# Layer 3's windowed-attention block: order of the weights' scaling, the norm's root and its product, the last steps and the leaving sequences

## The chip, the cores and the metric

The kernel runs on one core of one Trainium2 chip. The metric is the device time of the whole program in microseconds, as the median of several runs. Five engines run side by side, each through its own list of instructions in a fixed order: TensorE (PE: matrix products and transposes, with weight loads shown as PEld), VectorE (DVE), ScalarE (ACT), GpSimd (POOL) and SyncE (SP, which issues transfers). An instruction starts when the one ahead of it on its engine and the results that it needs are done.

## The reference

Four layers, each a half-step of a feed-forward block, an attention, and the feed-forward block again. The change lies in the feed-forward block of layer 3, called twice (ahead of that layer's attention and behind it). It works on 2 x 1024 tokens of 128 features, in two passes (DEPTH = 2):

```
h = shift_token(x)                              # features 64.. come from the token before
q, k, v = split(h @ wqkv)                       # 8 heads of 64
q, k = rotary_xpos(l2norm(q) * qs, l2norm(k) * ksc)
o = local_attention(q, k, v)                    # windows of 64 tokens, each sees the one before
x = x + o @ wo
h = shift_token(x)
h = (h - mean(h)) / sqrt(var(h) + 1e-05) * lg + lb
a, g = split(h @ w1 + b1)
x = x + (a * gelu(g)) @ w2 + b2
```

After it, the outer program adds half of the block's result to its own x.

## The kernel before

`l3_ffn(w3, tag, first, rb)` (line 1900) is one call of the block; `first` is true for the call ahead of the attention. A **unit** is one pass over one of four sequences of 512 tokens, so there are 8 units, and a unit has four **steps** of 128 tokens: 32 steps (`n_steps`). The loop at line 2231 runs `n` from -2 to 37. In each round it goes through six **places**, and at each place it runs one part for an earlier step, its lag:

| place | part (lag) | engines |
|---|---|---|
| 0 | `project` (0): products `p_qk`, `pv`; square `sq`, the rotary products `t`, the roots of the norms (10 small instructions on POOL), the scaled keys | PE, ACT, DVE, POOL |
| 1 | `to_features` (2): transposes `pt_qk`, copies `qT` (ACT) and `kT` (DVE) | PE, ACT, DVE |
| 2 | `exponentials` (4): eight exponentials with sums `sm` | ACT, DVE |
| 3 | `weights` (3): scores `ps3`, mask `s`, row maximum `nm` | PE, DVE |
| 4 | `with_values` (6): product `po3`, copy `oT` | PE, DVE |
| 5 | `turn_weights` (5): transposes `pt3`, copy `PT` | PE, ACT |

`shares(n - 5)` (line 2049) scales the exponentials by the reciprocal of their sum on POOL (L2051); `turn_weights` needs its result. It stands at place 0, behind what `later` holds for that place.

`later` is a table written by hand: what a unit still has to do after its four steps, as (round counted from the unit's first step, place). The list `parts` (line 2213) fills it: `summed` (10, 2), `shifted` (10, 3), `centred` (11, 1), `squared` (11, in the middle of the exponentials), `variance` (12, 0), `spread_by_act` (12, in the middle of the exponentials), `normed` (13, 0), three `hidden` (13, 2), `close_unit` (14, 0) and `leave` (14, 1). `MIDST` is the key of what `exponentials` runs behind its third exponential.

The norm of a unit goes so. `variance` brings the sums of squares to `rs` (a copy on DVE) and takes the root in two POOL instructions (L230 and L233). `spread_by_act` multiplies the identity by `rs` in four ACT instructions, tile `dg`. `normed` multiplies `dg` by a matrix of equal numbers on PE (`pb`), which spreads the factors over the partitions, and one DVE instruction scales `h` by it. `hidden` multiplies `h` by `w1`, in three pairs of products (`pag`), each followed by a Gelu (`ge`, ACT) and a product (`hh`, DVE). `close_unit` multiplies `hh` by `w2` (`pz`).

PSUM is held in three pairs of banks (tag "d": `p_qk`, `pt_qk`, `ps3`, `pt3` and each `pag`) and two single banks (tag "m": `pv`, `pb`, `pm`, `pvar`, `po3`, `pz`, `pt_y`, `pt_z`), each tag in turn. PE's, ACT's and the named POOL instructions are kept in the order of the program; DVE's order inside these calls is chosen by the scheduler when the kernel is built.

Rounds 32 to 37 hold no `project`: they drain the lags. The last unit's own steps (`rest`, line 2243) follow the loop, in the first call spread between those of the attention.

A sequence leaves with `leave(b)` (line 2181): transposed back, added to x, and in the first call normalized for the attention by `leave_normed` (line 349). That puts three tasks on a chain: statistics, scaling to `y`, and after a gap counted in places (`gap`, here 3) the transposes `pt_y` (`turn`, line 319). `tick()` at the end of each place runs what is due.

Of the kernel before, what the change touches and what calls it, by code (L numbers as in the profile page):

```python
# [115 lines left out]
def tile_macaron(ctx, tc, x_in, const_in, vec_in, w0_in, ws_in, ws3_in, w2f_in, w3_in, out):  # L116
# [82 lines left out]
    def mm_in_order(dst, lhsT, rhs, start=True, stop=True):  # L199
        tc.keep_in_program_order(nc.tensor.matmul(dst, lhsT=lhsT, rhs=rhs, start=start, stop=stop))  # L200
# [130 lines left out]
    def chain(b):  # L331
        parts = deque()
        chains.append([b, clock[0], parts])
        return lambda gap, f, products=True: parts.append((gap, f, products))
# [7 lines left out]
    def tick(busy=False):  # L342
        clock[0] += 1
        for c in list(chains):
            while c[2] and clock[0] >= c[1] + c[2][0][0] and not (busy and c[2][0][2]):
                busy |= c[2][0][2]
                run(c)

    def leave_normed(b, spare, gap, pinned=False, start=1, to_route=True):

        st = []

        def scale():
            scaled(y, x, b, st[-1] if pinned != "parts" else st[0][1:], pinned is True)
            ready.add(b)

        if pinned == "parts":
            got, halves = statistics_in_parts(x, b)
            st.append(got)
            spare(start, halves[0], False)  # L360
            spare(1, halves[1], False)
            spare(2, scale, False)
        else:
            spare(start, lambda: st.append(statistics(x, b)), False)
            spare(1, scale, False)
        spare(gap, lambda: turn(b))
        if routed and to_route:
            spare(1, lambda: logits(b))
            if b % 2:
                first, second, third = route(b // 2)  # L370
                spare(1, first, False)
                spare(routed["gaps"][0], second)
                spare(routed["gaps"][1], third)
# [1521 lines left out]

    MIDST = 2.5

    def l3_ffn(w3, tag, first, rb):  # L1900
        with pool(tag) as sb, banks(tag + "ps", d=3, m=2):
            units = [(l, b) for l in range(2) for b in range(B)]
            n_steps = TB * len(units)
# [12 lines left out]
            def W(l, name):  # L1916
                return W3(w3, f"{name}{l}")
# [39 lines left out]
            def project(step):  # L1957
                u, t = step // TB, step % TB
                l, b = units[u]
                h = u_state[u]["hT"][:, ts(t, P)]  # L1960
                p = pair("p_qk")
                mm_in_order(p[:, 0:512], h, W(l, "wq"))
                mm_in_order(p[:, 512:1024], h, W(l, "wk"))
                pv = bank("m", "pv3")
                mm_in_order(pv, h, W(l, "wv"))

                sq = sb.tile([P, 16, 64], F32, tag="sq", name="sq")
                act(sq.rearrange("p h d -> p (h d)"), p, AF.Square)
                tab = W(l, "tab").rearrange("p (t f i d) -> p t f i d", t=TB, f=2, i=2)[:, t]
                t1 = sb.tile([P, 16, 64], F32, tag="t1", name="t1", bufs=3)  # L1970
                t2 = sb.tile([P, 16, 64], F32, tag="t2", name="t2")
                by_head = lambda v: v.rearrange("p (i h) d -> p i h d", i=2)
                over = lambda v: v[:, :, None, :].to_broadcast([P, 2, 8, v.shape[2]])
                p3 = p.rearrange("p (h d) -> p h d", d=64)
                vector.tensor_mul(by_head(t1), by_head(p3), over(tab[:, 0]))
                for half in range(2):
                    a, z = ts(half, 32), ts(1 - half, 32)
                    vector.tensor_mul(by_head(t2[:, :, a]), by_head(p3[:, :, z]), over(tab[:, 1, :, a]))
                rn = sb.tile([P, 16], F32, tag="rn", name="rn", bufs=6)
                vector.tensor_reduce(rn, sq, AX.X, ALU.add)  # L1980
                pool_in_order(nc.gpsimd.tensor_add(t1, t1, t2))  # L1981
                inverse_root(sb, rn, rn, "ir16", ALU.max, 1e-24, nc.gpsimd, pin=pool_in_order)
                pool_in_order(nc.gpsimd.tensor_mul(t1[:, 8:16, :], t1[:, 8:16, :], bcast(rn[:, 8:16], 64)))
                v = sb.tile([P, S], F32, tag="v", name="v", bufs=7)
                act_copy(v, pv)

                vb = sb.tile([P, S], F32, tag="vb", name="vb", bufs=6) if t else vbs[u % 2]
                nc.sync.dma_start(vb[64:128], v[0:64])
                if t:
                    nc.sync.dma_start(vb[0:64], s_state[step - 1]["v"][64:128])  # L1990
                s_state[step] = {"qk": t1, "rn": rn, "v": v, "vb": vb}
# [42 lines left out]
            def exponentials(step):  # L2034

                midst = later.pop((step + 4, MIDST), ())
                s, nm, rn = (s_state[step][v] for v in ("s", "nm", "rn"))
                sm = sb.tile([P, 8], F32, tag="sm", name="sm", bufs=2)
                for i in range(8):
                    si = s[:, i, :]  # L2040
                    h = 2 * (i % 4) + i // 4
                    act(si, si, AF.Exp, bias=nm[:, i : i + 1], scale=rn[:, h : h + 1], accum_out=sm[:, i : i + 1])
                    if i == 2:
                        for f, u in midst:
                            f(u)
                vector.reciprocal(sm, sm)
                s_state[step]["sm"] = sm

            def shares(step):
                s = s_state[step]["s"]  # L2050
                pool_in_order(nc.gpsimd.tensor_mul(s, s, bcast(s_state[step].pop("sm"), P)))  # L2051
# [102 lines left out]
            def hidden(u, c, at=whole):  # L2154
                l, b = units[u]
                a, n = HCH[c]
                h2, w1, m = u_state[u]["h2"][:, at], W(l, "w1"), at.stop - at.start
                if c == 0 and at.start == 0:
                    u_state[u]["hh"] = rb.tile([P, 3, S], F32, tag="hh", name="hh")
                pg, pa = two_banks("pag")  # L2160
                mm_in_order(pg[:n, :m], w1[:, HID + a : HID + a + n], h2)
                mm_in_order(pa[:n, :m], w1[:, a : a + n], h2)
                ge = tmp("ge")
                act(ge[:n, :m], pg[:n, :m], AF.Gelu, bias=W(l, "b1g")[:n, c : c + 1])
                vector.scalar_tensor_tensor(
                    u_state[u]["hh"][:n, c, at], pa[:n, :m], W(l, "b1a")[:n, c : c + 1], ge[:n, :m], ALU.add, ALU.mult
                )
# [13 lines left out]
            def leave(b, at=whole):  # L2181
                pt = bank("m", "pt_z")
                t0, n = at.start // P, (at.stop - at.start) // P
                for t in range(n):
                    transpose_in_order(pt[:, ts(t, P)], yT[:, b, ts(t0 + t, P)])
                tiles = slice(b * TB + t0, b * TB + t0 + n)
                xb = x[:, tiles, :].rearrange("p t d -> p (t d)")
                vector.scalar_tensor_tensor(xb, pt[:, : n * P], 0.5, xb, ALU.mult, ALU.add)
                if first:
                    leave_normed(b, chain(b), 3)  # L2190
                else:
                    nc.sync.dma_start(out[:, tiles, :], x[:, tiles, :])

# [16 lines left out]
            if first:  # L2210
# [2 lines left out]
            parts = [  # L2213
                (summed, 10, 2), (shifted, 10, 3), (centred, 11, 1), (squared, 11, MIDST), (variance, 12, 0),
                (spread_by_act, 12, MIDST),
                (normed, 13, 0), *((lambda u, c=c: hidden(u, c), 13, 2) for c in range(3)), (close_unit, 14, 0),
                (lambda u: leave(units[u][1]) if units[u][0] else None, 14, 1),
            ]
            later, last = {}, len(units) - 1
            for u in range(len(units)):  # L2220
                for f, after, place in parts[: -1 if u == last - 1 else None] if u < last else ():
                    if u == last - 1 and f is close_unit:
                        after, place = 13, 5
                    if u == last - 1 and f is spread_by_act:
                        f, place = spread, 2
# [3 lines left out]
            if first:  # L2229
                later.setdefault((8, 1), []).append((scale_layer, 1))  # L2230
            for n in range(-2, n_steps + 6):
                for place, (part, lag) in enumerate((
                    (project, 0), (to_features, 2), (exponentials, 4), (weights, 3), (with_values, 6), (turn_weights, 5)
                )):
                    for f, u in later.pop((n, place), ()):
                        f(u)
                    if place == 0 and 0 <= n - 5 < n_steps:
                        shares(n - 5)
                    if 0 <= n - lag < n_steps:
                        part(n - lag)  # L2240
                    tick()
            assert not later, later
            rest = [attended, mean, variance, spread, normed]
# [15 lines left out]
    with pool("ws") as wp:  # L2259
# [9 lines left out]
        with pool("l2x") as l2x:  # L2269
# [20 lines left out]
            with ExitStack() as first_layer:  # L2290
# [3 lines left out]
                with pool("l1v", side="right") as vb:  # L2294
# [4 lines left out]
                    project, roots, unit_norm = projection(xb, seqs)  # L2299
# [206 lines left out]
```

## Time and profile before

| | us |
|---|---|
| median of 3 runs (2608.64 to 2609.08) | 2608.88 |
| the profiled run's own time | 2606.24 |
| its span, first to last instruction | 2604.3 |
| PE busy in the span | 2236.7 (86%) |
| DVE busy | 1771.5 (68%) |
| ACT busy | 1334.8 (51%) |
| POOL busy | 945.4 (36%) |

The mean granted TensorE clock is 0.909. Times of instructions are read from the span's start. The first call's first projection of a full pipeline is at about 1555 us, its last `pag` of the loop at 1883 us; the second call's loop has its last `pag` at 2570 us. PE's busy time comes from matmuls whose ends are modelled, since they are pipelined; so one may seem to start a little before the one ahead of it ends. "Idle before" is the time for which an engine stood ahead of an instruction, and the name behind the arrow is what released it.

### The profile page before, as it was taken

The page shows a single profiled execution, that of the slowest core. Times are in us where ns is not written, and L with a number is a line of the kernel's source. Part 1 is how long each engine was busy: PE and PEld are TensorE (multiplying, and loading weights), DVE is VectorE, ACT ScalarE, POOL GpSimd, SP SyncE. Part 2 cuts the span into 40 slices and gives each one's busy share as a digit, 9 for nine tenths or more (in the row PEclk, how much of TensorE's full clock was granted, in tenths as well). Part 3 has the DMA queues.
Part 4 walks back from the last instruction along what each step waited for, and adds up shares of the span by engine and source line. Part 5 has one row for each costly group of instructions (what it writes and reads, how often), then busy time and mean ns, then how long its engine had stood idle before and what let it go on. Part 6 is the DMA issues. An engine that isn't in the chain of part 4 may idle for free.

```text
span 2604.3 us, 50971 instructions
## 1 busy us (share of the span) xinstructions
PE 2236.7 (86%) x19070; PEld 1276.6 (49%) x19070; DVE 1771.5 (68%) x4755; ACT 1334.8 (51%) x3271; POOL 945.4 (36%) x1519
## 2 busy tenths in 40 slices
PE   5578679988778998988768868999889999799997
PEld 2246334443344444458647845555533333456555
DVE  3755667777466777755655579888557775788874
ACT  4056205444443544434425338887615555588884
POOL 2023113233233222333422368777310000787761
PEclk9789789899689999889978879999889999899999
DMA  3052000000000000037325721110000000110100
GB/s 150 0 170 92 1 0 2 2 1 2 1 1 1 2 2 5 17 128 238 106 83 159 252 84 28 24 24 21 3 1 1 1 1 1 29 28 22 24 22 13
DMA packets 40142, 113.21 MB, mean 43 GB/s; under 512 B 7064, under 2 KB 16536, under 8 KB 39384
## 3 DMA queue, kind: packets, MB, share of 16 engines
q1 hardware_dynamic: 36520, 100.94, 12.2%
q0 software_dynamic: 2944, 6.04, 1.1%
q8 instruction: 151, 2.47, 0.4%
q10 hardware_dynamic: 432, 2.98, 0.3%
q14 instruction: 95, 0.78, 0.1%
HBM read 79.78 MB, written 15.47 MB: 37 GB/s over the span
## 4 chain that ended last, share of the span: by engine, by line
PE 59%; DVE 18%; POOL 11%; ACT 6%; issue 4%; DMA 2%; SPq 0%; POOLq 0%; DVEq 0%; ACTq 0%
PE pk_at L200 11%; PE po_at L200 6%; PE pa L200 4%; PE pq_at L200 4%; DVE t L184 3%; PE pz L200 3%; PE pag L200 3%; PE pe L200 3%; PE po L200 2%; PE idle L200 2%; PE pt L197 2%; DVE y L184 2%; POOL t L1981 2%; PE pg L200 2%; PE p_qk L200 2%
## 5 line engine op out<-in xcount | busy, mean ns | idle before, releaser
L940 ACT ACTIVATE PT<-pk_at 128x512 f32<-128x512 f32 (+3 forms) x768 | 335.3, 488 | 377.6 <-PE pq_at L200 240.3
L200 PE MATMUL pk_at<-qx,km 32*128 32x512 f32 (+3 forms) x1536 | 400.6, 559 | 5.9 <-ACT PT L940 3.0
L184 DVE CUSTOM_DVE_ANT_0 s<-pq_at,cst 128x384 f32<-128x384 f32 (+3 forms) x512 | 249.3, 487 | 98.9 <-PE pq_at L200 46.2
L200 PE MATMUL pq_at<-km,qT 32*128 32x128 f32 (+3 forms) x1024 | 274.6, 504 | 15.6 <-DVE nm L184 12.5
L1923 ACT ACTIVATE s<-s,nm,rn 128x128 f32<-128x128 f32 x512 | 245.7, 483 | 4.4 <-DVE nm L184 4.2
L943 POOL TENSOR_SCALAR_AFFINE_SELECT PT<-PT 128x256 f32<-128x256 f32 x256 | 104.7, 411 | 383.5 <-ACT PT L940 382.3
L200 PEld LDWEIGHTS pk_at<-qx,km 32*128 32x128 f32 x1536 | 146.9, 191 | 155.0 <-issue 90.8
L200 PE MATMUL po_at<-PT,vh 128*32 128x128 f32 (+3 forms) x2432 | 203.3, 393 | 3.8 <-POOL PT L943 3.7
L184 DVE TENSOR_REDUCE nm<-pq_at 128x1 f32<-128x512 f32 x256 | 164.7, 684 | 52.5 <-PE pq_at L200 51.1
L184 DVE TENSOR_TENSOR t<-p_qk,w 128x512 f32<-128x512 f32 (+1 forms) x192 | 155.1, 861 | 53.5 <-ACT sq L1923 51.1
L1981 POOL TENSOR_TENSOR t<-t,t 128x1024 f32<-128x1024 f32 x64 | 151.2, 2362 | 55.9 <-DVE t L184 45.1
L200 PE MATMUL pq_at<-km,t 32*128 32x512 f32 x512 | 163.7, 657 | 0.1
L200 PE MATMUL p_qk<-w,hT 128*128 128x512 f32 x256 | 135.2, 654 | 18.1 <-DVE hT L184 9.2
L2051 POOL TENSOR_TENSOR s<-s,sm 128x1024 f32<-128x1024 f32 x64 | 121.5, 1899 | 63.1 <-DVE sm L184 62.1
L200 PEld LDWEIGHTS po_at<-PT,vh 128*32 128x32 f32 x2432 | 54.1, 110 | 169.9 <-issue 121.8
L233 POOL TENSOR_TENSOR ln_r<-ir,minus_half 128x4 f32<-128x4 f32 x60 | 62.0, 1034 | 202.4 <-DVE ir L184 200.5
L200 PEld LDWEIGHTS pq_at<-km,qT 32*128 32x128 f32 x1024 | 110.4, 190 | 43.6 <-DVE nm L184 23.1
L324 ACT COPY yT<-pt_y 128x512 f32<-128x512 f32 x56 | 32.7, 585 | 181.5 <-PE pt_y L197 181.2
L197 PE MATMUL pt<-ident,s 128*128 128x128 f32 x640 | 94.0, 294 | 31.1 <-POOL s L2051 28.5
L1585 POOL DMA_INDIRECT xg<-yd,come x60 | 57.4, 957 | 174.3 <-PE pt_x L197 74.3
L184 DVE SCALAR_TENSOR_TENSOR y<-pe,g,y 128x128 f32<-128x128 f32 x240 | 80.8, 348 | 30.7 <-PE pe L200 24.5
L197 PE MATMUL pt_y<-ident,y 128*128 128x128 f32 x224 | 48.6, 344 | 60.6 <-DVE y L184 47.2
(444 smaller groups left out, 5301.8 us busy)
## 6 DMA issues: line engine op xcount, KB each, us to landing
wf<-in_w2f_dram SPq DMA_DIRECT2D x45, 836.0 KB, 4.7
vb<-v SPq DMA_DIRECT2D x112, 128.0 KB, 2.3
w<-in_w2f_dram SPq DMA_DIRECT2D x15, 836.0 KB, 8.7
skew<-qe SPq DMA_DIRECT2D x16, 512.0 KB, 4.9
rel<-skew SPq DMA_DIRECT2D x64, 128.0 KB, 3.4
od<-o SPq DMA_DIRECT2D x60, 64.0 KB, 5.3
w<-in_w_dram SPq DMA_DIRECT2D x1, 3200.0 KB
w<-in_w_dram SPq DMA_DIRECT2D x12, 173.0 KB, 9.0
```

Source lines behind the costliest of these rows:

```text
L184: i = op(*args, **kw)
L197: return nc.tensor.transpose(dst, src, ident[: src.shape[0], : src.shape[0]])
L200: tc.keep_in_program_order(nc.tensor.matmul(dst, lhsT=lhsT, rhs=rhs, start=start, stop=stop))
L233: pin(nc.gpsimd.tensor_tensor(dst, v, minus_half[:, :n], ALU.pow))
L324: by_order(nc.scalar.copy(yT[:, b, :], pt))
L940: by_order(nc.scalar.activation(PT[:, i, q0:], pk[:, q0:], AF.Exp, scale=SC8))
L943: nc.gpsimd.affine_select(d, d, pattern=[[0, 2], [1, P]], base=0, channel_multiplier=-1, compare_op=ALU.is_ge, fill=0.0)
L1585: nc.gpsimd.indirect_dma_start(xT[s], None, yds[k][:, :], bass.IndirectOffsetOnAxis(ap=come[:, i : i + 1], axis=0))
L1923: tc.keep_in_program_order(nc.scalar.activation(*args, **kw))
L1981: pool_in_order(nc.gpsimd.tensor_add(t1, t1, t2))
L2051: pool_in_order(nc.gpsimd.tensor_mul(s, s, bcast(s_state[step].pop("sm"), P)))
```

## The change

There are six edits, all in or for `l3_ffn`.

1. `shares(n - 5)` is run ahead of what `later` holds for place 0, so ahead of `variance` and its root.
2. `normed` gets a key of its own, `BEHIND`: it runs inside `project`, behind its three products; in a round without `project`, at the end of place 0.
3. `exponentials` runs `squared` behind the third exponential as before, and `spread_by_act` behind the fourth.
4. In the rounds from 32 on, `turn_weights` is run at place 4 and `with_values` at place 5.
5. `leave_normed` is called with a gap of 9 places, not 3.
6. `BEHIND = 0.5` is defined.

```diff
-    MIDST = 2.5
+    MIDST, BEHIND = 2.5, 0.5
...
                 pv = bank("m", "pv3")
                 mm_in_order(pv, h, W(l, "wv"))
+                for f, v in later.pop((step, BEHIND), ()):
+                    f(v)
...
-                    if i == 2:
+                    if i == (2 if midst and midst[0][0] is squared else 3):
                         for f, u in midst:
                             f(u)
...
                 if first:
-                    leave_normed(b, chain(b), 3)
+                    leave_normed(b, chain(b), 9)
...
-                (normed, 13, 0), *((lambda u, c=c: hidden(u, c), 13, 2) for c in range(3)), (close_unit, 14, 0),
+                (normed, 13, BEHIND), *((lambda u, c=c: hidden(u, c), 13, 2) for c in range(3)), (close_unit, 14, 0),
...
             for n in range(-2, n_steps + 6):
+                ends = [(with_values, 6), (turn_weights, 5)]
                 for place, (part, lag) in enumerate((
-                    (project, 0), (to_features, 2), (exponentials, 4), (weights, 3), (with_values, 6), (turn_weights, 5)
+                    (project, 0), (to_features, 2), (exponentials, 4), (weights, 3), *ends[:: 1 if n < n_steps else -1]
                 )):
+                    if place == 0 and 0 <= n - 5 < n_steps:
+                        shares(n - 5)
                     for f, u in later.pop((n, place), ()):
                         f(u)
-                    if place == 0 and 0 <= n - 5 < n_steps:
-                        shares(n - 5)
                     if 0 <= n - lag < n_steps:
                         part(n - lag)
+                    elif part is project:
+                        for f, u in later.pop((n, BEHIND), ()):
+                            f(u)
                     tick()
```

## The prediction

> **What bounds the kernel now.** I read the busy time by stretch first. The change touches only the two calls of `l3_ffn` (about 1512 to 1900 us and 2217 us to the end), and in both a unit of four steps takes 42.05 us.
>
> ```profile
> core 0: us, PE busy (x) PEld busy (x) DVE busy (x) ACT busy (x) POOL busy (x), PEclk, DMA share, GB/s
> 1656.00:1698.00 42.00, 40.68 (x390) 24.91 (x384) 36.45 (x51) 34.73 (x93) 31.20 (x56) 1.00 0.10 23
> ```
>
> TensorE is busy for 40.68 of 42.00 us at full clock. So a unit ends when PE has done its list, and only what opens or closes a gap on PE counts: 1.32 us per unit can be won at most. The chain that ended last, in order of time, shows what releases PE there:
>
> ```profile
> 1664.66 1.88 POOL s L2051
> ...
> 1666.59 1.09 PE pt L197 x8
> ...
> 1671.42 2.41 DVE t L184 x3
> ...
> 1673.97 3.67 PE pag L200 x8
> ```
>
> PE waits for the scaled weights (`s`, L2051), then for the projections' readers (`t`) before `pag`. The timeline of that stretch (start, duration, idle before) gives the rows for the sum:
>
> ```profile
> 1663.62 1.04 POOL L233 TENSOR_TENSOR rs<-ir,minus_half 128x4 f32<-128x4 f32 x1
> ...
> 1664.63 1.90 POOL L2051 TENSOR_TENSOR s<-s,sm 128x1024 f32<-128x1024 f32 x1
> ...
> 1665.71 1.27 ACT L1923 ACTIVATE dg<-ident,rs 128x128 f32<-128x128 f32 x4
> ...
> 1666.59 1.09 PE L197 MATMUL pt<-ident,s 128*128 128x128 f32 x8 [0.72 <-POOL s L2051]
> ...
> 1666.78 0.68 DVE L184 COPY kT<-pt_qk 128x512 f32<-128x512 f32 x1
> ...
> 1667.51 1.02 PE L200 MATMUL pb<-dg,onesm 128*128 128x512 f32 x2
> ...
> 1668.37 1.88 PE L200 MATMUL p_qk<-w,hT 128*128 128x512 f32 x4
> ...
> 1669.27 0.99 ACT L1926 COPY PT<-pt 128x1024 f32<-128x1024 f32 x1
> ...
> 1670.34 1.02 ACT L1923 ACTIVATE sq<-p_qk 128x1024 f32<-128x1024 f32 x1
> ...
> 1670.61 0.74 DVE L184 SCALAR_TENSOR_TENSOR h<-h,w,pb 128x512 f32<-128x512 f32 x1
> ...
> 1671.40 2.42 DVE L184 TENSOR_TENSOR t<-p_qk,w 128x1024 f32<-128x1024 f32 x3
> ...
> 1671.83 1.88 PE L200 MATMUL pag<-h,w 128*128 128x512 f32 x4
> ...
> 1673.97 3.67 PE L200 MATMUL pag<-h,w 128*128 128x512 f32 x8 [0.26 <-DVE t L184]
> ```
>
> The 1.32 us are 0.72 (weights), 0.26 (`pag`) and 0.34 (`pvar`). Note that `h` ends at 1671.35, in the shadow of `sq`, and that ACT has no pause from 1664.27 to 1670.26.
>
> **Part 1: weights ahead of the root (POOL).** POOL is free at 1663.26 (end of L1983's product), and `sm` is there since 1661.92. Now the weights run 1663.35 to 1665.25, 1.28 us earlier, and the root's two instructions 1665.34 to 1666.65, 1.99 later. PE can turn the weights as soon as `po` ends, 1665.87: the 0.72 us go. What is late next is `p_qk`. There are three pairs of banks, and a step takes four, so `p_qk` gets the pair of the `pt_qk` before it, which `kT`'s copy releases at 1667.46. `p_qk` starts at about 1667.55 instead of 1668.37.
>
> **Part 2: the root's product behind the projections (PE, DVE).** `pb` takes 0.87 us of PE from ahead of `p_qk` to behind `pv`. Together: 1667.55 + 1.72 + 0.87 + 0.87 = 1671.0 for `pt_qk`, which began at 1670.96 before. The gain of part 1 is already spent there, on the wait for `kT`.
>
> **Part 3: the spread after four exponentials (ACT).** `dg` waits for the root. The fourth exponential leaves ACT free at 1666.20; the root is there at 1666.65, so `dg` starts at about 1666.70: ACT stands for 0.5 us. Queued behind that wait are four exponentials, the copy `PT`, the square `sq`, the copies `v` and `qT`, the table load and the Gelu. `PT` moves from 1669.27 to 1669.78. `sq` follows 0.91 behind it (0.89 in the step before, 1661.38 to 1662.27), at 1670.69, and ends at 1671.71.
>
> **What it does to `h`.** In the changed program as built, VectorE holds, in this order: `nm`, the first product of `t`, then `h`, then the other two of `t`. Before, `h` stood ahead of all three. `t` never starts before `sq` has ended (1671.36 to 1671.40 here). So: `t`'s first product 1671.75 to 1672.95 (1.22 us by the groups by form), `h` until 1673.6, and `pag`, which reads `h`, at about 1673.72 instead of 1671.83. PE stands from 1672.0 to 1673.72. `pag`'s twelve matmuls take 5.42 us unbroken (row at 2535.93 in the last unit), end 1679.14 against 1677.64: **+1.5 us per unit**. Behind `pag` PE has no wait before 1701.19, so nothing takes this back; the Gelu and `hh` keep ahead of `pz` (before by 1.4 us). Cheaper bound: if `dg` never waits, `sq` ends at 1671.18, and the same steps give +1.0. Dearer bound: +2.0, if the root is 0.5 us later still. I take 1.5, since every term has a row. Steps with both projections and `pb` occur for units 0 to 4, in two calls: 10 x 1.5 = **+15 us** (10 to 20).
>
> The weights pass only the root's two instructions on POOL, and the moved steps issue no DMA, so SP's queue stays as it is. The two transfers of `v` follow its copy, and are read six steps later.
>
> **Part 4: drain of the first call, and the leaving sequences.** The dear place is the step before the drain:
>
> ```profile
> 1823.61 1.04 POOL L233 TENSOR_TENSOR ln_r<-ir,minus_half 128x4 f32<-128x4 f32 x1
> ...
> 1824.69 1.12 DVE L184 TENSOR_SCALAR y<-x,ln_mv,ln_r 128x128 f32<-128x128 f32 x4 [3.99 <-POOL ln_r L233]
> ...
> 1825.09 1.24 PE L197 MATMUL pt_y<-ident,y 128*128 128x128 f32 x4 [5.09 <-DVE y L184]
> ...
> 1826.85 0.68 DVE L184 COPY oT<-po 128x512 f32<-128x512 f32 x1
> ```
>
> With the gap 9 instead of 3 `pt_y` goes one step later, and `p_qk` no longer stands behind it: it runs at 1819.85. But the wait moves. `pm` takes the bank of the `po` before it, free only after `oT` (1827.53), which stands behind `y` on DVE. So PE waits 5.1 us before `pm`, and queued behind it are `pt_qk`, `ps` and `po`. What is won is on DVE: `t` starts at 1827.6 instead of 1830.19, and POOL's chain with it (2.6 us). Next, the weights in front of the root: `pm` and `pt_qk` run slow until 1831.0 (1.72 each), then `qT`'s copy, three exponentials, the square (1833.0 to 1833.6) and five exponentials until 1836.0, so `sm` is there at 1836.5; the weights run 1836.7 to 1838.6 (before 1840.61 to 1842.51); `pt` 1838.65, `po` until 1840.7, the root 1838.7 to 1840.0, `dg` until 1841.3, `pb` 1841.4, `h` until 1843.1, `pag` 1843.25 to 1848.65. Before it ended at 1853.45: -4.8. In the last steps `po` goes behind `pt`; `pvar` still starts at the same distance, `pag` gains 0.1, and `pz` ahead of the last `po` 0.4. **-5.3 us** in all. Bounds: -8 (the whole 5.09 wait, and the slow clock behind it), 0 (each wait turns up again). The leavings inside the attention that follows show no wait of PE before `pt_y` (1935.45): 0, within 1 either way.
>
> **Part 5: drain of the second call.** There is no `pt_y`. Weights end 1.28 earlier, at 2530.3, but `po` now stands between `pt` and `pb`, and `dg` ends 2.0 later, at 2533.0: `pb` at 2533.6 (2533.38 before), `pag` 0.5 earlier thanks to the clock, then 0.15 and 0.4 as above: **-1.1 us** (-3 to +1).
>
> **The clock.** PE stands for 1.75 us before `pag`. Does it come back slow?
>
> ```profile
> 1563.85 1.09 PE L197 MATMUL pt<-ident,s 128*128 128x128 f32 x8 [1.70 <-POOL s L2051]
> ...
> 1842.57 1.97 PE L197 MATMUL pt<-ident,s 128*128 128x128 f32 x8 [3.02 <-POOL s L2051]
> ```
>
> After 1.70 us eight transposes take 1.09, after 3.02 us 1.97, and the next product 1.71 (2533.38) instead of 1.02. After a wait of 2.23 us (1876.30) the `po` rows are slow too. So the step lies between 1.7 and 2.23, and I take 0, with +1.6 per unit as the other end. [...]
>
> **Sum.** 15 - 5.3 - 1.1 = +8.6 us. The profiled run took 2606.24 us (span 2604.3 and 1.94 around it), 2.6 under the median 2608.88; taken from the median: **2617.5 us**.
>
> **Rivals.**
> - *The wait is only taken away (faster).* `pag` starts when PE is ready for it, 1672.0, and not when `h` is. Then a unit wins 0.2 (twelve at 5.42 end 1677.4); with no wait for `kT` either, up to 1.0. -10 x 0.2 - 6.4 = -8.4: 2600.5. It decides if `t`'s first product starts before 1670.0. For it: `p_qk` ends 0.8 us earlier. Against: `sq` stands behind ACT's unbroken row. 0.11.
> - *The drain gives nothing.* The stall goes from `pt_y` to `pm` in full: +15, 2624. For it: `oT` is the same row. Against: `t` and POOL's chain don't wait for `pm`. 0.15.
> - *PE comes back slow ten times:* 1.6 x 10 more, 2633. The gap is near 1.73 us (2560.58), where `pvar` kept its 1.05. 0.07.
> - *The unit's loss is half* (root early, `h` sooner): 0.7 a unit, 2609.5. 0.12.
>
> **How the numbers follow.** The forecast has 0.55, and its own range is 2612 to 2623. No change means within 0.2%, 5.2 us, about what a measurement here can tell: 2603.7 to 2614.1. The half loss and a little of the forecast fall in it, 0.16; faster 0.11, the first rival; slower 0.73. Range 2607 to 2627: it takes in the drain's rival and the half loss, and leaves out the first rival and the slow clock, 0.18.
>
> **What would show it.** Right: in a unit, the wait of `pt` for `s` gone, a wait of about 0.6 before `p_qk`, about 1.75 before `pag` with `h` as releaser, `dg` idle 0.5 for `rs`, units of 43.5 us, and `pm` at about 1827 (shifted by five units' loss, some 7.5 us) waiting for `oT`. Wrong: `pag` without wait for `h`, or units under 42.

## The result, and the profile after

| | before | after |
|---|---|---|
| median of 7 runs each, side by side, us | 2608.88 (2603.35 to 2611.57) | 2618.92 (2615.58 to 2624.02) |
| ratio, 95% interval | | 1.0042, 1.0032 to 1.0053 |
| the profiled run, us | 2606.24 | 2619.29 |
| PE, DVE, ACT, POOL busy, us | 2236.7, 1771.5, 1334.8, 945.4 | 2237.6, 1777.1, 1333.7, 945.3 |

The changed kernel is slower by 0.42%, 10 us; the forecast was 8.6. PE's work is the same and no engine's grew by more than 0.4%. So what is lost is waiting, and the page's list of costliest groups names the place. Its last two columns are busy time and mean of one, then the idle time of the engine just ahead of the group and what ended it:

```profile
L200 PE MATMUL pag<-h,w 128*128 128x512 f32 (+3 forms) x204 | 94.2, 615 | 17.7 <-DVE h L184 17.7
```

TensorE stands 17.7 us ahead of `pag`, and all of it is ended by `h` on VectorE; before it was 4.2 us in all, 1.7 of it ended by `h`. A steady unit in the busy time by stretch, 43.4 us instead of 42.05 and at full clock:

```profile
core 0: us, PE busy (x) PEld busy (x) DVE busy (x) ACT busy (x) POOL busy (x), PEclk, DMA share, GB/s
1655.00:1698.40 43.40, 40.97 (x384) 25.10 (x383) 36.66 (x51) 34.78 (x92) 31.21 (x57) 1.00 0.10 22
```

The chain of waits in that unit, in order of time (start, us, what). It no longer runs over POOL's `s` and `pt`, but over ACT's row and two VectorE instructions:

```profile
1664.65 1.82 ACT s L1923 x8
1666.47 0.98 ACT PT L1926
1667.45 0.93 ACT sq L1923
...
1668.40 1.22 DVE t L184
1669.63 0.67 DVE h L184
```

The timeline of the same step (start, duration, work, idle before):

```profile
1662.70 1.06 PE L197 MATMUL pt<-ident,s 128*128 128x128 f32 x8
...
1663.37 1.28 ACT L1923 ACTIVATE dg<-ident,rs 128x128 f32<-128x128 f32 x4 [0.26 <-POOL rs L233]
...
1664.33 1.99 PE L200 MATMUL p_qk<-w,hT 128*128 128x512 f32 x4 [0.57 <-DVE kT L184]
...
1667.02 1.02 PE L200 MATMUL pb<-dg,onesm 128*128 128x512 f32 x2
...
1668.40 1.22 DVE L184 TENSOR_TENSOR t<-p_qk,w 128x1024 f32<-128x1024 f32 x1 [0.31 <-ACT sq L1923]
...
1669.55 0.73 DVE L184 SCALAR_TENSOR_TENSOR h<-h,w,pb 128x512 f32<-128x512 f32 x1
...
1670.43 5.39 PE L200 MATMUL pag<-h,w 128*128 128x512 f32 x12 [1.51 <-DVE h L184]
```

`pt` no longer waits for `s`; `p_qk` waits 0.57 for `kT`, `dg` 0.26 for the root, and `pag` 1.51 for `h`. `pb` was done by 1668.04, yet `h` started at 1669.55: it stood behind `t`'s first product.

To compare kernels stage by stage I take the time from the start of one `pag` to the start of the next; the opening runs from a call's first `p_qk` to its first `pag`. "After, again" is a second profile of the changed kernel, from a later run, and "gap alone" an experiment told below.

| stage, us | before | after | after, again | gap alone |
|---|---|---|---|---|
| first call: opening | 115.72 | 117.49 | 118.98 | 115.70 |
| four units | 168.21 | 173.65 | 173.71 | 168.22 |
| last unit to the drain's first `pag` | 49.75 | 45.05 | 44.95 | 44.90 |
| to the drain's second `pag` | 35.43 | 36.59 | 37.58 | 35.28 |
| attention, to the next `p_qk` | 334.28 | 336.78 | 333.54 | 336.18 |
| second call: opening | 108.70 | 111.89 | 110.61 | 109.35 |
| four units | 168.22 | 175.26 | 173.74 | 168.22 |
| drain's first `pag` | 41.56 | 41.01 | 41.07 | 41.55 |
| drain's second `pag` | 34.36 | 34.71 | 34.83 | 34.36 |
| to the end | 33.99 | 35.47 | 35.56 | 33.98 |

The openings, the attention and the first drain's second `pag` differ by 1 to 3 us between two profiles of one kernel; units and the drains' first `pag` repeat to 0.1 us, apart from the second call's first unit in "after", which is 1.6 us longer (below). I rest on these, and on the ratios.

### The profile page after: what moved, and what is told of

It is laid out like the page before. It is cut to its first block, busy times and chain, and to the rows that moved or that the text cites. A ratio compares the mean times of both kernels' runs of the same rounds, so it can differ in the third digit from the quotient of the medians.

```text
span 2617.4 us, 50964 instructions
## 1 busy us (share of the span) xinstructions
PE 2237.6 (85%) x19070; PEld 1276.9 (49%) x19070; DVE 1777.1 (68%) x4755; ACT 1333.7 (51%) x3271; POOL 945.3 (36%) x1519
## 4 chain that ended last, share of the span: by engine, by line
PE 56%; DVE 20%; ACT 9%; POOL 7%; issue 4%; DMA 3%; SPq 0%; POOLq 0%; ACTq 0%; DVEq 0%
PE pk_at L200 11%; PE po_at L200 6%; PE pq_at L200 4%; PE pag L200 4%; DVE t L184 3%; PE pa L200 3%; PE pz L200 3%; ACT s L1923 3%; PE po L200 3%; PE pe L200 2%; DVE y L184 2%; PE p_qk L200 2%; DVE s L184 2%; ACT sq L1923 2%; PE pg L200 2%
## 5 line engine op out<-in xcount | busy, mean ns | idle before, releaser
L200 PE MATMUL pag<-h,w 128*128 128x512 f32 (+3 forms) x204 | 94.2, 615 | 17.7 <-DVE h L184 17.7
```

## The experiments

The kernels ran on several chips, on which the kernel before took 2609 to 2622 us; in the profiles the first call began between 1509 and 1530 us. So totals are given as ratios to runs of the kernel before on the same chip; the unit is the length that most units of the profile have. Names beginning with a are the changed kernel with one thing put back or moved, and with b the kernel before with one thing added.

| kernel | unit, us | ratio to before, 95% interval |
|---|---|---|
| before | 42.05 | |
| edit 1 alone (b_shares) | 43.55 | 1.0053, 1.0039 to 1.0067 |
| all but edit 2 (a_product_first) | 42.53 | 1.0000, 0.9988 to 1.0012 |
| all but edit 1 (a_root_first) | 43.04 | 1.0049, 1.0036 to 1.0061 |
| all (after, again) | 43.43 | 1.0036, 1.0020 to 1.0052 |
| all, `h` ahead of `t` (pin_h) | 42.56 | 1.0011, 1.0002 to 1.0020 |
| all, product ahead of `pv` (a_between) | 42.36 | 1.0006, 0.9994 to 1.0019 |
| all but edit 4 (a_order_back) | 43.43 | 1.0040, 1.0027 to 1.0053 |
| edit 5 alone (b_gap) | 42.05 | 0.9973, 0.9963 to 0.9984 |
| edit 4 alone (b_drain) | 42.06 | 1.0018, 1.0009 to 1.0028 |
| edits 4 and 5 (b_gap_drain) | 42.05 | 1.0009, 0.9997 to 1.0021 |
| edit 5, and 1 in the drains (b_gap_sh32) | 42.05 | 0.9982, 0.9971 to 0.9993 |
| edit 5, and 1 in the second drain (b_gap_sh2) | 42.07 | 0.9976, 0.9964 to 0.9989 |

### What the unit loses

**pin_h**: `h` and the instructions of `t` pinned in the order of the program, in the steps that hold both. The excerpt shows the first of `t`'s instructions; the others, the sums `rn` and `h` are held in the same way.

```diff
+                behind = later.pop((step, BEHIND), ())
+                hold = tc.keep_in_program_order if behind else lambda i: i
...
-                vector.tensor_mul(by_head(t1), by_head(p3), over(tab[:, 0]))
+                hold(vector.tensor_mul(by_head(t1), by_head(p3), over(tab[:, 0])))
```

> The changed kernel, with one thing put back: on VectorE the scaling of h stands ahead of t's three products again, in the five units of each call where both meet; no other engine's list changes. Theory (h stands behind t's first product, and the square comes late; both count): pb ends at 1667.9, so h runs 1668.05 to 1668.8 and t from 1668.85 instead of 1668.40; pag no longer waits for h, but its second pair waits for t until about 1671.4, where it now starts at 1672.2. A unit takes 42.6 us instead of 43.41, and the time is about 2611 (10 x 0.8 less than 2618.9). Rival 1 (h's place is no matter, the late root sets pag): units stay at 43.4, 2619. Rival 2 (h's place is all of the loss): units at 42.05 or less, 2605 or less.

Measured: 42.56, and 1.0011. That is the theory's 42.6, and neither rival's. The place of one 0.73 us instruction in VectorE's list is worth 0.85 us a unit. The rest is that `t` now waits for `h`, and that the second pair of `pag` then waits for `t`:

```profile
1681.09 0.75 DVE L184 SCALAR_TENSOR_TENSOR h<-h,w,pb 128x512 f32<-128x512 f32 x1
1681.75 2.41 DVE L184 TENSOR_TENSOR t<-p_qk,w 128x1024 f32<-128x1024 f32 x3
...
1684.31 1.95 PE L200 MATMUL pag<-h,w 128*128 128x512 f32 x4 [0.37 <-DVE t L184]
```

**a_between**: the product runs behind `p_qk` and ahead of `pv`. The scheduler puts `h` ahead of `t` by itself.

```diff
+                for f, v in later.pop((step, BEHIND), ()):
+                    f(v)
                 pv = bank("m", "pv3")
                 mm_in_order(pv, h, W(l, "wv"))
-                for f, v in later.pop((step, BEHIND), ()):
-                    f(v)
```

> The changed kernel with the root's product one place further ahead: behind p_qk, but ahead of pv. Theory: nothing of PE's is later than now, but pb is done 0.9 us earlier, VectorE holds h ahead of t's three products again and runs it in the shadow of the square; t starts when the square is done, as it does now. pag's first pair starts behind pt_qk, its second when t has ended: units of 42.2 us, about 2 us under the changed kernel in the first call per two units, 11 to 12 us under it in all (10 units x 1.2). Rival 1 (t, not h, sets pag): 43.4. Rival 2 (as with h pinned): 42.56.

Measured: 42.36, between the 42.2 expected and pin_h; 9.7 us under the changed kernel on the same chip. In one step of its timeline the square runs from 1669.66 to 1670.67, `h` from 1670.10 to 1670.84 and `t` from 1670.83; `pag` starts at 1671.04 without a wait, and only its later products wait for `t`, 0.45 us. So the place of `h` costs no more, and what is left over the kernel before (0.31) fits the later square; no run takes that away alone.

**a_product_first**: edit 2 undone.

```diff
-                (normed, 13, BEHIND), *((lambda u, c=c: hidden(u, c), 13, 2) for c in range(3)), (close_unit, 14, 0),
+                (normed, 13, 0), *((lambda u, c=c: hidden(u, c), 13, 2) for c in range(3)), (close_unit, 14, 0),
```

> The changed kernel with edit 2 undone: the root's product stands ahead of the projections again, the rest stays (weights ahead of the root, dg behind the fourth exponential). Theory: h goes back ahead of t on VectorE without a pin; pb waits about 0.3 us for dg, p_qk starts 1.2 us later, but the square stands behind ACT's own list until 1667.45 anyway, so t is not later; pag's second pair starts at about 1671.0 instead of 1672.2. A unit takes 42.2 us, the time is about 2607. Rival (the product behind the projections saves PE time, so that undoing it costs): units over 43.4, above 2619.

Measured: 42.53, and no difference from before. The unit is shorter than the changed kernel's, as expected, but by 0.9 and not 1.2 us, since `pb` waited 0.94 us for `dg` and not 0.3, and the square came behind `p_qk`.

**a_root_first**: edit 1 undone.

```diff
-                    if place == 0 and 0 <= n - 5 < n_steps:
-                        shares(n - 5)
                     for f, u in later.pop((n, place), ()):
                         f(u)
+                    if place == 0 and 0 <= n - 5 < n_steps:
+                        shares(n - 5)
```

> The changed kernel with edit 1 undone: the root ahead of the weights again, the product still behind the projections, dg behind the fourth exponential. Theory: pt waits some 0.7 us for s again, hidden for the most part in p_qk's wait for kT; dg finds its root ready and the square comes 0.3 us earlier; h still stands behind t's first product. A unit takes 43.1 us; the time is about 2616 to 2618, as the first call's drain loses some 1 us of its gain. Rival (the weights in front are the whole loss, since the root is late): units at 42.1, about 2606.

Measured: 43.04 (43.1 expected). The total was worse than expected, no better than the changed kernel's: its second drain took 43.17 us to the first `pag` instead of 41.01. So the late root is not the whole loss in the unit, and the rival falls.

**b_shares**: the reverse of that edit, in the kernel before.

> The kernel before with edit 1 alone, in all rounds: the weights ahead of the root; the root's product still ahead of the projections, dg behind the third exponential. Theory: pt's wait of 0.72 us goes, but dg waits about 1 us for the root, pb waits for dg ahead of p_qk, and the square and t come 0.5 to 1 us later: units of 42.6 to 42.9 instead of 42.05; both drains gain 1.0 (weights 1.28 earlier). 4 to 7 us over before. Rival (the wait is only taken away): units of 41.4, 7 us under before.

Measured: 43.55, worse than the theory's 42.6 to 42.9, and 1.0053. The timeline says where the estimate was short:

```profile
1665.15 1.28 ACT L1923 ACTIVATE dg<-ident,rs 128x128 f32<-128x128 f32 x4 [0.73 <-POOL rs L233]
...
1666.49 1.13 PE L200 MATMUL pb<-dg,onesm 128*128 128x512 f32 x2 [0.94 <-ACT dg L1923]
...
1674.08 1.10 PE L200 MATMUL pag<-h,w 128*128 128x512 f32 x2 [1.19 <-DVE t L184]
```

The wait of 0.72 for `s` turned into 0.73 on ACT, 0.94 on PE ahead of `pb`, and 1.19 ahead of the second pair of `pag`. So putting the weights in front costs the unit 1.50 by itself. With the weights in front, edit 3 (`dg` behind the fourth exponential) takes 1.02 of that away (43.55 to 42.53; the drains' edits leave the unit as it is), and edit 2 adds 0.88 again (42.53 to 43.41), by `h`'s place on VectorE. But these prices don't add up one by one: edits 2 and 3 without edit 1 cost 0.99 (a_root_first), and all three together 1.37. Neither edit 2 nor edit 3 was run alone.

### What the drains win and lose

**b_gap**: one number.

```diff
-                    leave_normed(b, chain(b), 3)
+                    leave_normed(b, chain(b), 9)
```

> The kernel before with edit 5 alone: the gap of 9 places. Theory: it is the whole of the first drain's gain and costs nothing elsewhere. Units 42.05; from the last full unit's pag to the one in the drain (steps 28 to 33 of the first call) 46.4 us, where before took 49.74; from there to the next pag 35.4 as before (b_gap_drain: 35.98); second call as before (41.55 and 34.36). 3.4 us under before. Rival (the stall only moves to pm): 49.7, no difference.

Measured: 44.90 where 46.4 was expected (before 49.75), then 35.28; 6.9 us under before. The rival (the stall only moves) falls, though the wait itself is there as predicted, at `pm`, and as long as it was at `pt_y`:

```profile
1828.10 2.05 PE L200 MATMUL pm<-h,onesm 128*128 128x512 f32 x2 [5.10 <-DVE nm L184]
...
1840.48 1.09 PE L197 MATMUL pt<-ident,s 128*128 128x128 f32 x8 [0.66 <-POOL s L2051]
```

The last row tells where the gain comes from. In the kernel before, this `pt` came 44.57 us behind the last unit's `pag`, after a wait of 3.02 us (the prediction's row at 1842.57); now it comes at 42.07, since `t` and POOL's chain are earlier. That is 2.50 us. And behind the wait of 0.66 `pt`, `pb` and `pt_qk` take 1.09, 1.06 and 1.04 us, where they took 1.97, 1.92 and 1.91 behind the 3.02, at a granted clock of 0.50 (1842.57 to 1847.00). That is the other 2.35.

No kernel of the study is faster than this one edit; the two below that add to it can't be told from it.

**b_drain**: edit 4 alone.

```diff
-                    (project, 0), (to_features, 2), (exponentials, 4), (weights, 3), (with_values, 6), (turn_weights, 5)
+                    (project, 0), (to_features, 2), (exponentials, 4), (weights, 3), *ends[:: 1 if n < n_steps else -1]
```

> The kernel before with edit 4 alone: from round 32 on pt ahead of po. Theory: po (1.8 us of PE) no longer fills the wait for the scaled weights, PE stands 4.4 instead of 3.0 us ahead of pt and po follows at slow clock. First call 49.7 and then 36.0 to 36.6 (before 35.43), second call 44.1 (before 41.55) and 35.5 (before 34.36): 4 to 5 us over before. Rival (as predicted: pvar at the same distance, pz earlier): 0.5 us per call under before.

Measured: 50.28 and 36.68 in the first call, 44.01 and 35.52 in the second; 1.0018, 5.6 us over before. In the second call's drain PE now stands while POOL scales the weights, and `po` follows ahead of `pb`, both as slow as at a granted clock of 0.50 (the first row of `po` takes 0.48 us, as in the kernel before at 1876.30, granted 0.50, and 0.34 at 2282.51, granted 1.00; `pb` takes 2.08, and 1.02 in the prediction's row at full clock):

```profile
2533.48 1.97 PE L197 MATMUL pt<-ident,s 128*128 128x128 f32 x8 [4.43 <-POOL s L2051]
2535.38 0.48 PE L200 MATMUL po<-PT,vb 128*64 128x64 f32 x4
...
2537.28 2.08 PE L200 MATMUL pb<-dg,onesm 128*128 128x512 f32 x2
```

Before, the wait was 3.02 us, since `po` filled the rest, and `pb` followed `pt` at once.

**b_gap_drain**: edits 4 and 5.

> The kernel before with edits 4 and 5 alone: the gap of 9 places, and the other order of the last two places in the rounds from 32 on; nothing else is changed. Theory: units stay at 42.05; the stall of 5.1 us before pt_y turns up before pm, but t runs 2.6 us earlier; without the weights in front of the root the first call's drain gains about 3.5 instead of 5.0, and some 1 is given back in the next steps: 2605 to 2607. Rival 1 (drain and gap are the loss of the later steps): no gain or a loss, 2609 to 2611. Rival 2 (all of the 5 us stays): 2603.

Measured: 46.37 and 35.98 in the first call, 44.09 and 35.49 in the second. The first drain gains 3.4 and gives 0.5 back, near the 3.5 and 1 expected; but the second call's drain, which the expectation left out, loses 5.2 with its end, and no gain is left (1.0009).

**b_gap_sh32** and **b_gap_sh2**: edit 5, and edit 1 for some rounds.

```diff
+                    if place == 0 and n >= n_steps and 0 <= n - 5 < n_steps:
+                        shares(n - 5)
                     for f, u in later.pop((n, place), ()):
                         f(u)
-                    if place == 0 and 0 <= n - 5 < n_steps:
+                    if place == 0 and n < n_steps and 0 <= n - 5 < n_steps:
                         shares(n - 5)
```

> The kernel before with edit 5, and with edit 1 in the rounds from 32 on alone; units and the order of the last two places as before. Theory: what the runs show to gain, without what they show to cost. Units 42.05; first call 45.1 (before 49.74) and 35.4; second call 40.6 (before 41.55) and 34.4. 5.5 us under before, ratio 0.998. Rival (the earlier weights need pt ahead of po to gain anything): as with the gap alone, 3.4 under before.

> The kernel before with edit 5, and edit 1 only in the second call's rounds from 32 on, where no y runs beside the weights. Theory: units 42.05; first call as with the gap alone (44.9 and 35.3), second call 40.5 and 34.4 instead of 41.55 and 34.36: 1 us under the gap alone, 6 to 8 us under before, ratio 0.997. Rival (the second call's gain is lost behind the drain): as with the gap alone.

Measured: second drain 40.51 and 40.52 (40.5 expected, before 41.56), so the weights in front are worth 1.0 there up to the first `pag`; the stages behind it give half of that back (34.47 and 34.49, 34.48 and 34.41, against 34.36 and 33.98). In the first drain they are worth nothing: 45.14, against 44.90 with the gap alone. `pt` comes 1.6 us earlier (40.47 instead of 42.07 behind the last unit's `pag`), but `pb` stays (43.18 and 43.00): it waits 1.61 us for `dg`, which waits for the root. In total neither can be told from the gap alone.

**a_order_back**: the changed kernel with edit 4 undone.

> The changed kernel with edit 4 undone: in the drains po ahead of pt again. Theory: units 43.41; first call 45.1 from the last unit's pag to the drain's, then 36.3 (changed kernel: 36.59; po fills the wait for the weights, but y still waits on VectorE while POOL scales them); second call 40.5 and 34.5 (41.01 and 34.71). 1 to 2 us under the changed kernel. Rival (with the weights in front, the order of pt and po matters no more): no difference.

Measured: 44.95 and 35.49, then 41.70 and 33.89; 1.0040, the same as the changed kernel. The 1 to 2 us expected can't be seen in the total; the drains' second `pag` came about 1 us earlier in both calls, the second call's first `pag` 0.6 later. How much edit 4 costs with the weights in front stays open.

**after_again**: the changed kernel unchanged.

> The changed kernel as it is, once more, beside the next three. Its first profile was 2.5 us longer in the attention behind the first call, 3.2 in the opening of the second call and 1.6 in that call's second unit than the kernel before. Theory (matmuls slowed for a while in that one profile): units 43.41 as before, the opening of the second call (first p_qk to first pag) about 109.5 us instead of 111.9, and all units of the second call alike; 10 us over before. Rival (the change does it): the same three places are longer again.

Measured: 1.0036; attention 333.55, opening 110.61, all four units of the second call 43.42 to 43.45. So the attention and the long unit of the first profile are not there in every run, as the theory says; of the opening's 3.2 us, 1.9 are there again. But it was no single accident: a_order_back has the same three places long again (attention 336.91, opening 112.01, unit 44.98). The long unit is the clock's work (below). The attention takes 333.3 to 336.9 us over all the profiles, with 334.28 in the kernel before and 336.18 with the gap alone, so nothing can be read from it.

## Why the prediction was right, and where it was not

**The unit** (+1.5 predicted, +1.37 measured). Each step showed: no wait for `s`, 0.57 ahead of `p_qk` (0.6), and 1.51 ahead of `pag` for `h` (1.75). ACT's stop for the root was 0.26 and not 0.5, and that is what is missing in the wait (0.24). pin_h shows that `h`'s place on VectorE is worth 0.85 of the loss; in a_between, where `h` runs beside the square, 0.31 is left, which fits the later square, as argued. The two openings lose 1.8 to 3.3 and 1.9 to 3.2 us by the two profiles, a unit's loss each and a little more.

**The first drain, to its first `pag`** (-4.8 predicted, -4.69 and -4.80 measured). The number was right; one of its steps was not, so the exactness is partly luck. The wait went from `pt_y` to `pm` as foretold:

```profile
1829.94 2.04 PE L200 MATMUL pm<-h,onesm 128*128 128x512 f32 x2 [5.09 <-DVE nm L184]
```

The profile names `nm`, a VectorE instruction of 0.15 us right behind `oT` (1829.11 to 1829.79), where the prediction named `oT`. What failed is the term for the weights: the sum credited part of the gain to the weights in front of the root, and b_gap has the whole of it (-4.85) without them. With them `pt` comes 1.8 us earlier still, but `po` and a wait of 0.62 for `dg` stand between it and `pb` (43.09 behind the last unit's `pag`, 43.00 with the gap alone).

**The last steps of the first call** (-0.5 predicted, +1.2 and +2.2 measured). Here the step "`po` goes behind `pt`; `pvar` still starts at the same distance, `pag` gains 0.1" failed, in two ways. `po` behind the last `pt` stands in the way of `pb`: that `pt` ends at 32.83 behind the drain's first `pag`, and `pb` starts at 34.63; with the gap alone it follows `pt` at once (32.80). And an instruction that no edit touches became longer. The timeline of after, and of the gap alone:

```profile
1862.68 2.21 DVE L184 TENSOR_SCALAR y<-x,ln_mv,ln_r 128x128 f32<-128x128 f32 x2
1862.90 1.90 POOL L2053 TENSOR_TENSOR s<-s,sm 128x1024 f32<-128x1024 f32 x1 [0.89 <-DVE sm L184]
...
1866.66 1.10 PE L200 MATMUL pm<-h,onesm 128*128 128x512 f32 x2 [1.35 <-DVE h L184]
```

```profile
1860.25 0.55 DVE L184 TENSOR_SCALAR y<-x,ln_mv,ln_r 128x128 f32<-128x128 f32 x2
1860.50 2.06 POOL L2051 TENSOR_TENSOR s<-s,sm 128x1024 f32<-128x1024 f32 x1 [0.92 <-DVE sm L184]
```

In after, the last of the four `y` lasted until POOL's product was done, 1.99 us instead of 0.34, and `pm` came 1.25 later (20.93 instead of 19.68 behind the `pag` before it). With the gap alone `y` kept its 0.34, and POOL's product took 2.06 instead of 1.90.

Up to the second `pag` the loss over the gap alone splits so: edit 4 adds 0.70 (b_gap_drain, 35.98 against 35.28), and the other edits, the long `y` among them, 0.61 more (36.59). Of the 1.25 at `pm` only part arrives: a_order_back has the long `y` too, and is 0.21 over the gap alone. The 0.99 between the two profiles of the changed kernel is `pb` by itself, 1.13 us in one and 2.08 in the other; in the first the granted clock was 0.50 over `pt` (1876.60 to 1878.50) and 1.00 over `pb` (1880.36 to 1881.49).

**The second drain** (-1.1 predicted). Its first `pag` gained 0.5, and the stages behind it lost 1.8 to 2.0. Edit 4 alone loses 1.2 and 1.5 in these two stages (b_drain). From the start of the last `pag` to the end the kernel takes 15.1 us (before 13.8), and all of that difference is in one row, before and after:

```profile
2590.46 6.49 PE L200 MATMUL pag<-h,w 128*128 128x256 f32 x24
```

```profile
2602.31 7.81 PE L200 MATMUL pag<-h,w 128*128 128x256 f32 x24
```

The waits ahead of it are the same (0.90 us ahead of `pb`), but its matmuls stand 0.43 us apart for the first 11 in after and for the first 5 before, and then 0.22. So the clock was slow for longer; the mean granted clock over that stretch is 0.68 after and 0.82 before. Why it was is not shown: a_order_back, with edit 4 undone, has 7.76, and the gap alone 6.49.

**The clock** (0 predicted): right for the steady units, where twelve matmuls of `pag` took 5.39 us behind the wait of 1.51, at a granted clock of 1.00. In the opening of the second call the wait was longer, 2.34 us in "after" and 1.82 in the second profile, where the same twelve took 5.39 again:

```profile
2330.99 6.99 PE L200 MATMUL pag<-h,w 128*128 128x512 f32 x12 [2.34 <-DVE h L184]
```

That one slow return (mean granted clock 0.77 over the row), 1.6 us as the prediction priced it, is the whole of the long unit (45.01 instead of 43.41). The prediction's "the step lies between 1.7 and 2.23" did not hold, as the last section shows.

**The rivals.** "The wait is only taken away" is refuted by the 17.7 us ahead of `pag`. "The drain gives nothing" was wrong for the first `pag`, though the next steps returned a quarter to nearly half of it. "The unit's loss is half" falls with 1.37 a unit. Loss in the units (11 us over the eight that the marks enclose, by the second profile) and gain in the first drain came out as in the sum.

**The total** (+8.6 predicted, +10.0 measured, 8.3 to 13.8 by the interval). That it came so near is partly luck. By the stages of the two calls, the attention left out, the change costs 15.2 us in one profile and 15.1 in the other: units and openings 17.4 and 16.2, the first drain -4.7 and -4.8, the steps behind it +1.2 and +2.2, the second drain +1.3 and +1.5. The terms behind the first drain were 4 to 5 us dearer than predicted. Why the medians show 5 us less than the stages (1.3 at least, by the interval) stays open; there is only one profile of the kernel before to take the stages from.

## What to carry to other kernels

Before an order is changed by hand on some engines, look at the built order of the engine that nobody fixes: here one instruction of 0.73 us behind its neighbour cost 0.85 us in every unit, more than the wait that the change removed. A wait is worth filling: in b_drain `po` went from ahead of PE's wait for POOL to behind it, the wait grew from 3.02 to 4.43 us, and the second drain's first `pag` came 2.45 later. And edits that arrive together should be run apart: one of these five was worth 5 us by its stages and 7 by its median, and the others together cost more than that.

## What the runs showed of the hardware

In the first call's drain a VectorE `y` of 0.34 us (TENSOR_SCALAR, 128x128, f32) and a POOL product of 1.90 us (128x1024, f32) begin together (0.01 us apart in after, 0.04 in b_gap), and one of the two took longer. In after, after_again, pin_h, a_product_first, a_between, a_order_back, b_shares and b_gap_sh32 POOL's product began 17.17 or 17.18 us behind the drain's `pag` (18.12 in b_shares), and `y` took 1.99 or 2.00. In b_gap, b_gap_drain, b_drain, a_root_first and b_gap_sh2 it began at 17.19 or 17.20; `y` took 0.34, and the product 2.05 or 2.06. So a start some 0.02 us earlier went with 1.25 us at `pm` (20.93 in after, 19.68 in b_gap). The first eight are just the runs in which edit 1 stands in that drain, so the long `y` comes with edit 1; why POOL begins 0.02 us earlier there is not shown, nor is what makes one of the two long. Which of them issued first can't be read from the recorded starts. In the trace of after the long `y` doesn't show as idle time of VectorE: it is one instruction of 1.99 us, its recorded start (1862.89) lies even ahead of the product's (1862.90), and it ends at 1864.89, the product at 1864.80.

The length of PE's wait does not by itself tell whether the clock comes back slow. The same eight transposes in the opening of the second call, behind the same wait, before (granted clock 0.50) and after (1.00):

```profile
2285.58 1.97 PE L197 MATMUL pt<-ident,s 128*128 128x128 f32 x8 [1.92 <-POOL s L2051]
```

```profile
2286.98 1.09 PE L197 MATMUL pt<-ident,s 128*128 128x128 f32 x8 [1.92 <-POOL s L2053]
```

At this place the wait is 1.91 to 1.93 us in eleven of the profiles; six came back slow, five at full clock. In a_root_first twelve `pag` took 5.39 us behind 2.26. And in the second drain of "after" the eight transposes took 1.27 us behind 3.03, at a mean granted clock of 0.82, and the `po` that followed ran at 0.50 (before, behind 3.02: 1.97 us at 0.50). So these profiles give no single step, neither the prediction's nor another.
